# Residual rows of the last twelve chunks fetched by three large transfers, and the second sequence's statistics split over two steps

## Chip, cores and metric

One core of one Trainium2 chip runs the whole program. The metric is the device time of one execution in microseconds, and the median of several runs is given. Beside it stands one execution taken by the hardware profiler, whose span runs from its first to its last instruction.

## What is computed

Two sequences of 2048 tokens with 256 features pass through a recurrent layer and then through an attention layer with mixtures of experts for values and outputs. Both are added to their inputs. Cut to what matters here:

```python
x = x + rnn(layernorm(x), Wi, bi, Wh, bh)            # x: (2, 2048, 256)
y = layernorm(x)
q, k = heads(y @ Wq), heads(y @ Wk)                  # 8 heads of 64
wv = topk_mask(y @ Ws, 2) * sigmoid(y @ Ws)          # 5 experts, 2 taken
v = einsum('bthe,btek->bhtk', wv, einsum('btd,edk->btek', y, Wv))
attn = softmax(q * scale @ k.T) @ v
out = x + einsum('bthe,bthk,ekd->btd', topk_mask(y @ Wd, 2), attn, Wo)
```

The `x` of the last line, the output of the recurrent layer, is what this text calls the residual. The change concerns how its rows come back from memory for that last addition, and where the mean and variance for `layernorm(x)` of the second sequence are taken.

## The kernel before

The first 130 us hold the recurrent layer. Its result goes to a scratch tensor in memory, `x1d`, as 16 chunks of 128 rows for each of the two sequences (`b` is the sequence, `c` the chunk).

Attention follows, from about 130 us to the end. A *unit* is one head and one block of 512 queries: 8 heads by 4 blocks by 2 sequences make 64 units. A unit has eight tiles of scores (256 keys by 512 queries, held as 128 x 1024), which are treated in four *steps* `T` of two tiles, so there are 256 steps. In a step PE makes two tiles of scores `s` (L636); ACT copies them to a ring of tiles `p0` (even tiles) and `p1` (odd tiles, nine buffers; L648); DVE keeps the running maximum `m` (L658 to L664). When a unit's scores are complete, PE turns the maximum (`pm`, L677), DVE reduces it (`mq`, L682, `reduce_max`), and PE spreads it again (`pt`, L691, `spread_max`). Six steps behind (`LAG`), the maximum is subtracted by POOL or DVE (L704), ACT takes exponentials in place (L707), PE multiplies by the values (`o`, L717, `products`), POOL issues a DMA that adds the odd tile of a pair onto the even one (L729, `fold`; after it the `p1` tile is not needed any more), and PE sums the folded tiles over the keys (`d`, L738, `sums`). `take` and `take_sums` bring `o` and `d` to SBUF (`os`), and `close` divides and applies the output gates (`po` L770, `den` L772, `pro` L783); `gather` adds a head's share to what the other heads gave, for the last head on POOL (L840) into a tile `y` that `fetch_y` has loaded from memory (L804).

All instructions are in an order that is written by hand: the loop over `T` at the end of the kernel calls the pieces of a step in fixed order, and three tables of closures (`before`, `first_behind`, `behind`) say what else is called in a step and in which of its places. The engines run beside each other, each in its own order, with semaphores between them. SP issues nearly all other DMAs, also in program order, so an issue that must wait holds up those after it.

Two things lie beside that stream:

- Statistics of the second sequence. In the steps T = 15, 19, ..., 43, `stats_late` takes mean and variance of two chunks (L179 and L180 on DVE, four instructions in all), both at the end of the step, in `behind`. The rows are loaded by `load_late` (L886) one or two steps before. Step T = 19 and its like is the last of a unit (T % 4 == 3); the next step begins with that unit's `turn_max` and `reduce_max`.
- The output. When the last head of a query block is complete, `turn_out` transposes a chunk of `y` (`py`, L853), ACT copies it (`yT`, L857 and L860), a tile `z` of 128 x 256 (three buffers) is taken, and SP issues the load of the residual rows into it (L862, 128 KB). `project_out` multiplies by the output weights (`pz`, L870), DVE adds `z` (L878), and SP stores the result (L879). `pz` lies in one of two PSUM buffers that it shares with `po` and other small tiles.

The last three units end in `drain()`, a fixed list of calls after the loop. It holds the tail of the exponentials and products (`tv` and `tu` are the first tiles of the last two units), and the output of chunks 2 to 15 of the second sequence, in which a load of `z` stands in SP's order among the stores of earlier chunks.

Of the kernel before, what the change touches and what calls it, by code (L numbers as in the profile page):

```python
# [8 lines left out]
F32 = mybir.dt.float32  # L9
# [11 lines left out]
def rnn_then_switchhead_kernel(  # L21
# [658 lines left out]
    def reduce_max(u):  # L680
        pm, mq = mx_of[u]
        nc.vector.tensor_reduce(mq, pm, AX.X, ALU.max)  # L682

    def spread_max(u):
        _, mq = mx_of[u]
        if spare:
            pt = other(f"pt{u}_").rearrange("p (s q) -> p s q", q=P)
        else:
            pt = misc([P, QS, P], f"pt{u}")
        for s in range(QS):  # L690
            nc.tensor.transpose(pt[:, s, :], mq[:, s : s + 1].to_broadcast([P, P]), ident)  # L691
        pt = pt.rearrange("p s q -> p (s q)")
        if u in top_of:
            top_of[u] = (pt, top_of[u][1])
            return
        top_of[u] = (pt, ap.tile([P, QB], F32, tag="top", name=f"top{u}"))
        nc.scalar.copy(top_of[u][1], pt)  # L697
# [150 lines left out]
    def turn_out(b, c):  # L848
        yf = y_of[b, c // QS][:, c % QS].rearrange("p e k -> p (e k)")
        py = other(f"py{b}_{c}")[:, : len(o_chunks) * P] if spare else misc([P, len(o_chunks) * P], f"py{b}_{c}")  # L850
        py = py.rearrange("p (k n) -> p k n", n=P)
        for k, (r0, m) in enumerate(o_chunks):
            nc.tensor.transpose(py[0:m, k, :], yf[:, r0 : r0 + m], ident)  # L853
        yT = yT_all[yT_of["n"] % 2]
        yT_of["n"] += 1
        full = sum(m == P for _, m in o_chunks)
        nc.scalar.copy(yT[:, 0:full, :], py[:, 0:full, :])  # L857
        for k, (r0, m) in enumerate(o_chunks):
            if m < P:
                nc.scalar.copy(yT[0:m, k, :], py[0:m, k, :])  # L860
        z = ap.tile([P, D], F32, tag="z", bufs=3, name=f"z{b}_{c}")
        nc.sync.dma_start(out=z, in_=x1d[c, :, b, :])  # L862
        yT_of[b, c] = (yT, z)

    def project_out(b, c, at_end=False):
        yT, z = yT_of.pop((b, c))
# [69 lines left out]
        late["c"].pop(0)()  # L936


    before, first_behind, behind = {}, {}, {}

    def at(table, T, f, *a):
        table.setdefault(T, []).append(lambda: f(*a))
# [34 lines left out]
    for b in range(1, B):  # L977

        T0 = (b - 1) * H * H_T + 2 * LAG + 3
        for c in range(NCH):  # L980
            T = T0 + c // 2 * U_T
            at(behind, T - 2 + c % 2, load_late, b, c)
            at(behind, T, stats_late, b, c)
        T0 += NCH // 2 * U_T
        for part in range(2):
            at(behind, T0 + 3, scales_late, b, part)
            T0 += U_T
        for c in range(NCH):
            T = T0 + c // 2 * U_T + c % 2
            at(behind, T - 2, load_late, b, c)  # L990
            at(behind, T, normalize_late, b, c)
            at(behind, T + 2, turn_late, b, c)
            at(behind if c % 2 else before, T + 3, logits_late, b, c)
        T0 += 2 * NCH + U_T
        for part in range(2):
            for half in range(2):
                at(behind, T0, gates, b, part, half, False)
                for k in range(E):
                    at(behind, T0 + 1 + k, gates_go_on)
                T0 += 2 * U_T  # L1000
        assert T0 <= b * H * H_T
# [25 lines left out]
    def drain():  # L1027


        w, v, u = len(units) - 3, len(units) - 2, len(units) - 1  # L1030
        tv, tu = HC * v, HC * u
        outs = [(B - 1, c) for c in range(NCH)]
        turned, projected = 2, 1

        def turn(n=1):
            nonlocal turned
            for _ in range(n):
                turn_out(*outs[turned])
                turned += 1

        def project(n=1):
            nonlocal projected
            for _ in range(n):
                project_out(*outs[projected])
                projected += 1

        spread_max(v)
        turn_max(u)
        subtract(tv + 6, True)
        subtract(tv + 7)  # L1050
        reduce_max(u)
        take_sums(w)
        exponential(tv + 5)
        project()
        spread_max(u)
        products(tv + 4)
        products(tv + 5)
        fold(tv + 2)
        fold(tv + 4)
        exponential(tv + 6)  # L1060
        exponential(tv + 7)
        subtract(tu, True)
        close(w)
        gather(w)
        turn()
        exponential(tu)
        subtract(tu + 1, True)
        exponential(tu + 1)
        subtract(tu + 7)
        subtract(tu + 2, True)  # L1070
        products(tv + 6)
        products(tv + 7)
        fold(tv + 6)
        turn()
        project()
        take(v)
        sums(tv, tv + 2, True, False)
        exponential(tu + 2)
        subtract(tu + 3, True)
        exponential(tu + 3)  # L1080
        subtract(tu + 4, True)
        project()
        products(tu)
        products(tu + 1)
        turn()
        fetch_y(v)
        fold(tu)
        subtract(tu + 5, True)
        exponential(tu + 4)
        turn()  # L1090
        project()
        products(tu + 2)
        products(tu + 3)
        fold(tu + 2)
        sums(tv + 4, tv + 6, False, True)
        take_sums(v)
        exponential(tu + 5)
        subtract(tu + 6, True)
        turn()
        project()  # L1100
        exponential(tu + 6)
        products(tu + 4)
        products(tu + 5)
        exponential(tu + 7)
        turn()
        fetch_y(u)
        project()
        close(v)
        gather(v)
        products(tu + 6)  # L1110
        products(tu + 7)
        take(u)
        project()
        sums(tu, tu + 2, True, False)
        sums(tu + 4, tu + 5, False, False)
        sums(tu + 6, tu + 7, False, True)
        take_sums(u)
        turn()
        turn()
        project()  # L1120
        turn()
        project()
        turn()
        close_last(u, outs[-QS - 2 :])

    with tc.manual_schedule():
        for T in range(NT):
            new = (2 * T, 2 * T + 1)
            sub = [t for t in (2 * (T - LAG + 1), 2 * (T - LAG + 1) + 1) if 0 <= t < 2 * NT]
            old = [t for t in (2 * (T - LAG), 2 * (T - LAG) + 1) if 0 <= t < 2 * NT]  # L1130
            u_old = (T - LAG) // U_T - 1
            done = (T - LAG) % U_T == 0 and 0 <= u_old < len(units)
            fresh = sub and sub[0] % HC == 0
            if done:
                take(u_old)
            if old:
                exponential(old[1])

            ss = [scores(t) for t in new]
            stage(new[0], ss[0])  # L1140
            if T % U_T == 0:
                stage(new[1], ss[1])
                if T > 0:
                    turn_max(T // U_T - 1)
                    reduce_max(T // U_T - 1)
                largest(new[1], ss[1])
            else:
                largest(new[1], ss[1])
                stage(new[1], ss[1])
            if fresh:  # L1150
                subtract(sub[0])
            if T % U_T:
                largest(new[0], ss[0])
            if fresh:
                subtract(sub[1])
            k = T - LAG
            first = T % U_T == 0
            if first and k > 0:
                fold(2 * (k - 1))
            if sub and not fresh:  # L1160
                subtract(sub[0])
            if not first and k > 0:
                fold(2 * (k - 1))
            if sub and not fresh:
                subtract(sub[1])
            for f in before.pop(T, []):
                f()
            for t in old:
                products(t)
            if 3 <= k and k % 2:  # L1170
                t = 2 * (k - 3)
                sums(t, t + 2, t % HC == 0, t % HC != 0)
            if sub:
                exponential(sub[0])
            for f in first_behind.pop(T, []) + behind.pop(T, []):
                f()
        assert not before and not behind and not first_behind
        scores_only.close()
        spare["pool"] = ctx.enter_context(tc.tile_pool(name="ps_z", bufs=4, space=PSUM))
        drain()  # L1180


# [44 lines left out]
```

## Time and profile before

| quantity | us |
|---|---|
| median of 3 runs (1567.87 to 1571.04) | 1567.89 |
| the profiled execution's own time | 1569.4 |
| its span, first to last instruction | 1567.6 |
| PE busy | 1512.6 (96%) |
| DVE busy | 1299.1 (83%) |
| POOL busy | 1287.7 (82%) |
| ACT busy | 1247.8 (80%) |
| statistics of the second sequence on DVE | between 232.4 and 378.6 |
| start of the first projection inside `drain()` | 1513.0 |
| last residual addition | 1564.32 to 1564.74 |

PE is the matrix engine, DVE the vector engine, ACT the scalar engine, POOL GpSimd, and SP the queue that issues DMAs. An engine's busy time is an average over stages. What a piece of work costs is read from the stage that it stands in: from the idle time that the profile puts just before an instruction, in brackets, with the engine that ended it.

### The profile page before, as it was taken

To read this page: it belongs to the slowest core of one execution; us is meant where nothing else is said; L and a number is where in the kernel's file an instruction comes from. 1 tells how busy PE (TensorE), PEld (TensorE's weight loads), DVE (VectorE), ACT (ScalarE), POOL (GpSimd) and SP (SyncE) were. 2 spreads that over 40 slices of the span, in tenths; PEclk is the share of its full clock that TensorE was granted. 3 is DMA by queue.
4 is the path that set the end of the run, shared out by engine and by line. 5 is a ranking of instruction groups with operands and counts; after the bars stand their busy time and mean duration, and the time that the engine had idled before them with its cause. 6 is when DMAs were issued, how large, how long until landed. Compare 5 with 4: busy or idle time off the path is not lost. (4 is left out here: it accounts for less than half of the span.)

```text
span 1567.6 us, 41503 instructions
## 1 busy us (share of the span) xinstructions
PE 1512.6 (96%) x17582; PEld 533.7 (34%) x17582; DVE 1299.1 (83%) x1811; ACT 1247.8 (80%) x1617; POOL 1287.7 (82%) x855
## 2 busy tenths in 40 slices
PE   6988899999999999999999999999999999999997
PEld 5984222222233333333223332222222222222233
DVE  7473799999988888888987779999999999999873
ACT  4674688888888888888887778888888888888882
POOL 3053699898999988999998778899999999999980
PEclk9999999999999999999999999999999999999999
DMA  5021377888889987888897767788888888888955
GB/s 167 1 109 32 102 153 189 186 187 176 181 174 188 177 180 161 173 171 175 171 202 155 163 159 181 170 178 179 176 179 178 176 176 170 176 174 176 197 117 149
DMA packets 86959, 254.09 MB, mean 162 GB/s; under 512 B 11952, under 2 KB 31216, under 8 KB 86768
## 3 DMA queue, kind: packets, MB, share of 16 engines
q0 software_dynamic: 43488, 164.65, 57.5%
q1 hardware_dynamic: 41648, 86.13, 16.5%
q8 instruction: 139, 2.28, 0.6%
q10 hardware_dynamic: 1632, 0.61, 0.1%
q14 instruction: 52, 0.43, 0.1%
HBM read 59.46 MB, written 50.33 MB: 70 GB/s over the span
## 5 line engine op out<-in xcount | busy, mean ns | idle before, releaser
L704 POOL TENSOR_TENSOR p<-p,top 128x1024 f32<-128x1024 f32 x378 | 1006.3, 2768 | 27.9 <-ACT top L697 27.4
L648 ACT COPY p<-s 128x1024 f32<-128x1024 f32 x512 | 511.7, 1013 | 139.8 <-issue 49.5
L707 ACT ACTIVATE p<-p 128x1024 f32<-128x1024 f32 x512 | 538.8, 1063 | 50.7 <-DVE p L704 41.9
L636 PE MATMUL s<-q,k 64*32 64x512 f32 x4096 | 501.6, 596 | 3.6 <-ACT p L648 2.4
L636 PE MATMUL s<-qs,k 64*32 64x512 f32 x4096 | 501.4, 596 | 3.3 <-ACT p L648 1.8
L717 PE MATMUL o<-p,v 128*32 128x512 f32 x4096 | 491.0, 597 | 3.2 <-DVE os L754 2.3
L658 DVE TENSOR_TENSOR m<-s,m 128x1024 f32<-128x1024 f32 x320 | 390.9, 1222 | 89.4 <-PE s L636 80.8
L729 POOL DMA_DIRECT2D p<-p x254 | 263.0, 1036 | 97.6 <-issue 42.4
L717 PEld LDWEIGHTS o<-p,v 128*32 128x32 f32 x4096 | 113.5, 109 | 299.4 <-issue 158.0
L636 PEld LDWEIGHTS s<-qs,k 64*32 64x32 f32 x4096 | 100.3, 105 | 154.6 <-ACT p L648 58.2
L636 PEld LDWEIGHTS s<-q,k 64*32 64x32 f32 x4096 | 100.2, 105 | 153.9 <-ACT p L648 59.9
L704 DVE TENSOR_TENSOR p<-p,pt 128x1024 f32<-128x1024 f32 x126 | 152.5, 1210 | 0.0
L738 PE MATMUL d<-p,ones 128*32 128x512 f32 x1032 | 135.0, 592 | 0.9 <-DMA p<-p 0.9
L658 DVE TENSOR_TENSOR m<-s,p 128x1024 f32<-128x1024 f32 x64 | 78.4, 1225 | 57.5 <-ACT p L648 57.0
L783 DVE TENSOR_TENSOR pro<-po,mr 128x1280 f32<-128x1280 f32 (+1 forms) x67 | 95.9, 1431 | 2.7
L620 DVE TENSOR_TENSOR xq<-xq,wp 128x1280 f32<-128x1280 f32 x60 | 89.2, 1487 | 2.3 <-DVE wp L618 0.2
L626 DVE TENSOR_REDUCE v<-xq 128x256 f32<-128x1280 f32 x60 | 88.5, 1476 | 0.0
L159 PE MATMUL pq<-xn2T,wq 128*32 128x512 f32 x512 | 63.2, 612 | 6.4 <-DVE rtd L427 6.4
L140 PE MATMUL pk<-xn2T,wk 128*32 128x512 f32 x512 | 61.5, 597 | 0.0
L837 POOL DMA_DIRECT2D yd<-pro x48 | 61.0, 1270 | 0.0
L738 PEld LDWEIGHTS d<-p,ones 128*32 128x32 f32 x1032 | 33.9, 110 | 77.8 <-issue 75.8
L396 POOL TENSOR_TENSOR x<-x,hvb 128x512 f32<-128x512 f32 x14 | 17.9, 1276 | 45.8 <-ACT hs L369 34.2
(179 smaller groups left out, 1493.5 us busy)
## 6 DMA issues: line engine op xcount, KB each, us to landing
p<-p POOLq DMA_DIRECT2D x254, 512.0 KB, 5.4
xq<-xvd SPq DMA_DIRECT2D x60, 640.0 KB, 4.6
yd<-pro POOLq DMA_DIRECT2D x48, 640.0 KB, 6.5
qs<-q SPq DMA_DIRECT2D x64, 128.0 KB, 4.5
yd<-pro SPq DMA_DIRECT2D x8, 640.0 KB, 5.9
y<-yd SPq DMA_DIRECT2D x8, 640.0 KB, 7.3
x<-in_x SPq DMA_DIRECT2D x16, 256.0 KB, 5.5
x1d<-x SPq DMA_DIRECT2D x16, 256.0 KB, 2.0
```

The lines of the kernel that those rows point to most:

```text
L159: nc.tensor.matmul(pq[at_col : at_col + 32, :], lhsT=wq[:, kc, h * DH + g : h * DH + g + 32], rhs=xn2T[:, kc, b, n * QB : (n + 1) * QB], s ...
L620: nc.vector.tensor_tensor(xq, xq, wp.unsqueeze(2).to_broadcast([P, 4, DH, E]), ALU.mult)
L626: nc.vector.tensor_reduce(v_of[i][:, 4 * part : 4 * part + 4, :], xq, AX.X, ALU.add)
L636: nc.tensor.matmul(ss[g : g + 32, o, :], lhsT=k_of[i][half, c, g : g + 32], rhs=q_of[i, n][o][half, :], start=True, stop=True, tile_positi ...
L648: nc.scalar.copy(p, ss)
L658: nc.vector.tensor_tensor(m, ss, ring[t - 1] if c == 1 else m, ALU.max)
L704: eng.tensor_tensor(p, p, top.unsqueeze(1).to_broadcast([P, 2, QB]), ALU.subtract)
L707: nc.scalar.activation(ring[t], ring[t], AF.Exp)
L717: nc.tensor.matmul(o_of[u][at_col : at_col + 32, :], lhsT=v_of[i][:, 2 * c + o, g : g + 32], rhs=ring[t][:, o, :], start=c == 0, stop=c == ...
L729: nc.gpsimd.dma_start(out=ring[t], in_=ring.pop(t + 1), accum_op=ALU.add)
L738: nc.tensor.matmul(den_of[u][32 * g : 32 * (g + 1), :], lhsT=ones32, rhs=ring[(t, t1)[g // 2]][:, g % 2, :], start=first, stop=last, tile_ ...
L783: nc.vector.tensor_tensor(dst, po[:, s : s + n, 0:DH].unsqueeze(2).to_broadcast([P, n, E, DH]), mr[:, s : s + n].unsqueeze(3).to_broadcast ...
```

## The change

Residuals: a new function `load_z` takes one buffer of the ring `p1` and loads four chunks of residual rows (512 KB) into it with one DMA. It is called three times in `drain()`: twice at its start, for chunks 4 to 7 and 8 to 11, and once after the second projection in the list, for chunks 12 to 15. `turn_out` uses a slice of such a tile where there is one, and takes a `z` tile and loads it as before otherwise (chunks 0 to 3 of this sequence and everything earlier). The buffers are those whose tiles are folded last: the three calls take the ones of the tiles folded in step 254, in step 255, and by the first `fold` in `drain()`. In the same list `fetch_y(v)`, the load of `y` for chunks 8 to 11, stands one turn and two projections earlier.

Statistics: a new table `between` has a place just before `largest(new[1], ...)`, and in the first step of a unit this is behind `reduce_max`. The even chunk of a pair is measured there in the step T of before (the last of a unit), the odd one there in the next step, behind the maximum of the finished unit.

The instructions of PE, ACT and POOL and their order are the same in both kernels. On DVE the statistics move; on SP twelve loads go, three come, and one moves.

```diff
@@ turn_out
-        z = ap.tile([P, D], F32, tag="z", bufs=3, name=f"z{b}_{c}")
-        nc.sync.dma_start(out=z, in_=x1d[c, :, b, :])
+        z = yT_of.pop(("z", b, c), None)
+        if z is None:
+            z = ap.tile([P, D], F32, tag="z", bufs=3, name=f"z{b}_{c}")
+            nc.sync.dma_start(out=z, in_=x1d[c, :, b, :])
         yT_of[b, c] = (yT, z)
+
+    def load_z(b, n):
+
+        z = ap.tile([P, QS, D], F32, tag="p1", bufs=RING[1], name=f"zz{b}_{n}")
+        nc.sync.dma_start(out=z, in_=x1d[n * QS : (n + 1) * QS, :, b, :].rearrange("c p d -> p c d"))
+        for s in range(QS):
+            yT_of["z", b, n * QS + s] = z[:, s, :]
@@ the table of the second sequence
             at(behind, T - 2 + c % 2, load_late, b, c)
-            at(behind, T, stats_late, b, c)
+            at(between, T + c % 2, stats_late, b, c)
@@ drain
+        load_z(B - 1, NQ - 3)
+        load_z(B - 1, NQ - 2)
         spread_max(v)
         turn_max(u)
         subtract(tv + 6, True)
...
         fold(tv + 6)
         turn()
+        fetch_y(v)
         project()
+        load_z(B - 1, NQ - 1)
         take(v)
         sums(tv, tv + 2, True, False)
...
         products(tu + 1)
         turn()
-        fetch_y(v)
         fold(tu)
@@ the loop over T
                 if T > 0:
                     turn_max(T // U_T - 1)
                     reduce_max(T // U_T - 1)
+                for f in between.pop(T, []):
+                    f()
                 largest(new[1], ss[1])
             else:
+                for f in between.pop(T, []):
+                    f()
                 largest(new[1], ss[1])
                 stage(new[1], ss[1])
```

More of the change, by code (lines that the diff above doesn't have):

```diff
@@ L936, in gates_go_on @@
         late["c"].pop(0)()
-    before, first_behind, behind = {}, {}, {}
+    before, between, first_behind, behind = {}, {}, {}, {}
     def at(table, T, f, *a):
@@ L1176, in rnn_then_switchhead_kernel @@
                 f()
-        assert not before and not behind and not first_behind
+        assert not before and not between and not behind and not first_behind
         scores_only.close()
```

## The prediction, on record before the changed kernel ran

> **What bounds the kernel now.** I read the page first, then the waits of each engine in the last 57 us, the timelines of DVE and SP there, the end of the chain, and then the groups and timelines of the steps with statistics beside units without them.
>
> ```profile
> PE 1512.6 (96%) x17582; PEld 533.7 (34%) x17582; DVE 1299.1 (83%) x1811; ACT 1247.8 (80%) x1617; POOL 1287.7 (82%) x855
> ```
>
> PE is the bound: in the middle a PE gap is time, and an idle DVE is not. So I look for PE's gaps in the two stages that the change touches, and for what stands between PE's last matmul and the end. The waits of PE from 1511 us on:
>
> ```profile
> PE po L770 <- DVE z L878: 2.5, 1, 2.5
> PE py L853 <- POOL y L840: 0.9, 1, 0.9
> PE pz L870 <- DVE den L772: 0.5, 1, 0.5
> PE pz L870 <- ACT yT L857: 0.4, 2, 0.2
> ```
>
> The first is at 1539.12: `po` needs the PSUM buffer of the projection of chunk 5, and DVE has not added the residual to it. DVE's timeline and SP's say why:
>
> ```profile
> 1526.41 1.21 DVE L704 TENSOR_TENSOR p<-p,pt__17190 128x1024 f32<-128x1024 f32 x1
> 1534.50 0.42 DVE L878 TENSOR_TENSOR z<-pz,z 128x256 f32<-128x256 f32 x1 [6.88 <-issue]
> 1538.63 0.42 DVE L878 TENSOR_TENSOR z<-pz,z 128x256 f32<-128x256 f32 x1 [1.76 <-DMA z<-x1d]
> ...
> 1522.55 4.30 SPq L879 DMA_DIRECT2D out<-z  x2
> 1526.95 1.15 SPq L862 DMA_DIRECT2D z<-x1d  x1
> 1528.20 0.98 SPq L804 DMA_DIRECT2D y<-yd  x1
> ```
>
> The projection of chunk 4 is done at 1528.3, but its residual, behind a store on SP, is only asked for at 1526.95 and takes 7.5 us: 1534.45. Everything behind it on DVE is late: the sums of L761, a subtraction (1535.65), two exponentials, `po`, the gated `pro`, and with it POOL's addition (1544.19 to 1547.10) that `py` waits for. The end of the chain is the same:
>
> ```profile
> 1561.80 2.33 DMA z<-x1d
> ...
> 1564.32 0.42 DVE z L878
> ```
>
> PE's last projection ends at 1562.90, yet the addition starts at 1564.32, on a residual asked for at 1561.80.
>
> In the steps with statistics, PE waits once a unit before it spreads the maximum:
>
> ```profile
> 255.75 0.65 PE L691 MATMUL pt<-ident,mq 128*128 128x128 f32 x4 [0.39 <-DVE mq L682]
> 253.09 0.42 DVE L179 BATCH_NORM_STATS2 stl<-xl 128x6 f32<-128x256 f32 x1
> 269.17 1.23 DVE L658 TENSOR_TENSOR m<-s,m 128x1024 f32<-128x1024 f32 x1 [0.66 <-PE s L636]
> 1407.50 1.23 DVE L658 TENSOR_TENSOR m<-s,m 128x1024 f32<-128x1024 f32 x1 [0.66 <-PE s L636]
> 1414.44 1.22 DVE L658 TENSOR_TENSOR m<-s,p 128x1024 f32<-128x1024 f32 x1 [0.77 <-ACT p L648]
> ```
>
> The four statistics instructions (from 253.09 to 254.25) stand ahead of `mq`, and `pt` waits 0.39 for it. The last two lines are a unit without statistics: no wait at `pt`, and DVE has two idle places, 0.66 before the maximum of the last step and 0.77 before the first maximum of the next unit. The windows between turned maxima:
>
> ```profile
> 252.85:273.58 20.73, 20.27 (x244) 5.82 (x236) 19.40 (x26) 17.84 (x21) 18.44 (x11) 1.00 0.88 210
> 1391.60:1411.91 20.31, 20.23 (x244) 5.81 (x237) 18.37 (x22) 17.65 (x21) 18.51 (x12) 1.00 0.87 176
> ```
>
> First length, then PE, PEld, DVE, ACT and POOL busy. PE's work is equal, the length differs by 0.42.
>
> [...] for 6.88 us DVE leaves L761 and L704 undone that need no residual. [...] The trace has 2.1 to 2.6 for a quiet residual and 4.1 for a quiet `y`, but up to 9.2 and 9.8 beside other traffic. [...] the trace has 424 for L878 and 406 for L179.
>
> **The change part by part.**
>
> *Residuals.* Out: twelve loads of 128 KB; in: three of 512 KB, the same bytes, into buffers that are free. SP gets 9 issues fewer (0.32 to 1.18 us each), which is off the path.
> When do they land? The first waits for the fold of step 254, issued at 1503.49 and landed 4.6 later, so for nothing; it goes behind the load of chunk 1, at 1512.6. The second waits for the fold of step 255 (1508.80 + 4.8 = 1513.6; I take 1514.5, as the first transfer runs beside it). Duration: a quiet 128 KB takes 2.3, a quiet 640 KB 4.1, so 512 KB about 3.7 (an estimate between these rows); beside traffic up to 9.8. I take 4 to 6: chunks 4 to 7 are there by 1518, chunks 8 to 11 by 1521, both before the first need at 1528.3. The third goes out behind a store at about 1522.9 and is needed after 1556.
> Then the 6.88, 1.76, 2.52 and later residual waits of DVE go. What is late next? PE up to 1536.57 has no gap above 0.2 and stays. After that:
> - `po` follows the projection of chunk 6 at once: -2.54. Its `os` is ready, since L761 moves to about 1531.6. The subtraction and two exponentials behind it end by about 1536, before the products that need them (1537.1; before, 1539.70).
> - The projection of chunk 7 waits 0.53 for the residual addition of chunk 6; gone.
> - `py` waits 0.93 for POOL. Now `pro` runs 1537.9 to 1539.4, POOL 1539.4 to 1542.3, and PE gets there at 1542.9: gone, with 0.6 to spare. POOL needs `y` of chunks 8 to 11, now asked for at about 1520.4 behind the transpose of chunk 3; with 9.8 us it lands at 1530.
> - The sums before that need the fold issued at 1529.77, which took 11.2 beside `y` and two residuals, to 1541.0. PE now wants it at about 1540.1. `y` and the residuals are no longer beside it, so 5 to 7 us, 1536; had it stayed at 11.2, it would take back 0.9.
> - From `py` on PE runs without gaps to its end, 4.0 earlier (1558.9), and the last addition follows 0.07 behind it, as at 1549.79, instead of 1.42: -1.35. `y` of the last unit is asked for behind the transpose of chunk 7 (1535.1) and needed at 1549.8.
> Sum: 2.54 + 0.53 + 0.93 + 1.35 = 5.35.
> What the new traffic costs: 1 MB between 1512.6 and 1520, with the folds issued at 1514.07 and 1516.83 and the residuals of chunks 2 and 3 (4.0 and 7.4 us), which are behind the large transfers on SP. Chunk 2 landed at 1520.1 and is added at 1522.11; chunk 3 at 1524.6, added at 1526.07; the first fold at 1519.4, summed at 1521.61. All have 1.5 to 2.2 us to spare, and the DMA is idle from 1514 to 1516. The extra is 1 MB at about 290 GB/s (108 GB/s at a DMA share of 0.37 after 1550), 3.6 us, of which 2 lie in that idle stretch. So the loss is between 0 and 1.6 past these margins for PE; below nothing is excluded, since nothing that PE waits for in that stretch comes earlier. I take 0.4.
>
> *Statistics.* The same 32 instructions. The even pair (0.42 and 0.18, and 0.65 to the next start as at 253.64 to 254.29) goes into the idle 0.66 before L658 in the last step. If it is over by some tenths, the maximum, ACT's copy and PE's next scores follow: at 414.75 a row of small instructions made that maximum late by about 0.97, and PE lost 0.73, so 0.24 is free. The odd pair goes into the 0.77 behind `mq`: 0.65 fits, and if not, DVE comes to the next idle place (0.66) a little later. Nothing of ACT or POOL waits for statistics; of SP only the load that reuses the tile, a step ahead of its need. So the waits at `pt` of eight units go: 0.38, six of 0.39, 0.73, sum 3.45. In the first of these the idle place is only 0.26 (227.78): 0.65 - 0.26 - 0.24 = 0.15 comes back; I take 0.2 for the other margins, 0.02 and 0.12 wide. Gain 3.1, between 1.5 (the even pair disturbs half as much) and 3.4.
>
> *Together:* 5.35 - 0.4 + 3.1 = 8.1 (rounded up from 8.05). Against the profiled span 1567.6 this is 1559.5, and for its own time 1569.4 it is 1561.3; the median of the runs shown, 1567.89, is 0.3 above the span, so 1567.9 - 8.1 = 1559.8.
>
> **The rivals.**
> 1. *The traffic takes the place of the late residual.* A fold or the residual of chunk 2 lands 2 to 4 us late, and PE stalls in 1521 to 1530. For it: a DMA share of about 1.0 from 1516 to 1522, one landing of 11.2. Against: the idle stretch. 1567.9 - 3.1 - (5.35 - 3) = 1562.4.
> 2. *The statistics only change place.* The margin of 0.01 before L658 does not hold, and PE waits at its scores instead of `pt`. For it: the row at 414.75. Against: there it was 1.72 us of instructions, not 0.65. 1567.9 - 4.95 = 1562.9.
> 3. *Slower.* SP stands at the second large transfer. Its issue waits for the fold of step 255 and for other completions of POOL's DMAs; if one of these is the fold issued at 1516.83 (landed at 1524.4), or the transfers crawl, the residual of chunk 2 goes out behind it. Each us that it lands after 1522.4 stops DVE, with the subtractions, exponentials and products behind it, by one us. It must land at 1530.5 to eat up the 8.1: 1524.4 plus 6. With 9.2 us it lands at 1533.6, cost 11.2: 1571.0. Against: only earlier folds can have had that buffer.
> 4. *The residuals still come late*, since the large transfers are held up but chunk 2 is not: the statistics alone, and a rest, 1565.
>
> **How the numbers follow.** Forecast 0.66; rival 1 0.15; rival 2 0.10; rival 3 0.04; rival 4 0.05. The range goes from both gains whole and half a us more (1567.9 - 8.8 - 0.5 = 1558.6, and below it to 1558.0 for waits that I have not summed) to the upper end of rivals 1 and 2, 1563.5. This kernel's measurement can tell about 0.2%, 3.1 us, from no change: faster means below 1564.8. That is the forecast and rivals 1 and 2 (0.91), less a little for stalls that add up: faster 0.90, same 0.06, slower 0.04.
>
> **What would show it.** Right: no residual wait above 0.5 on DVE after 1515; `po` directly behind `pz`; last addition within 0.1 of PE's end; units of about 20.3 from 232 to 398; no PE wait at `pt` there. Wrong: PE waits before `d` or `o` around 1520 to 1530, PE waits at L636 in those units, or an SP wait above 5 us at the second large load.

## The result, and the profile after

| | before | after |
|---|---|---|
| median of six runs on one chip, us | 1569.11 (1567.87 to 1571.04) | 1563.84 (1560.75 to 1564.61) |
| profiled execution's own time, us | 1569.4 | 1563.39 |
| its span, us | 1567.6 | 1561.6 |
| its mean granted clock | 0.997 | 0.995 |

The ratio is 0.9962 with an interval of 0.9949 to 0.9975: 6.0 us faster, 3.9 to 8.0 (the two medians differ by 5.3). The forecast was 8.1 faster, a little outside that interval, and its time of 1559.8 is 4.0 below the median measured. Of these 4.0, 1.2 is the kernel before itself, whose median was 1567.89 in the three runs shown ahead of the prediction and 1569.11 in six. The stated range ended at 1563.5, and the median of 1563.84 lies 0.3 above it; 0.9962 of the 1567.89 that it was reckoned from is 1561.9, inside the range. In what follows the differences count.

First PE's share of the span on the page of the changed kernel, then the list of all waits of PE in its end stage, from 1503 us on (engine, line, what it waited for: us in total, times, longest):

```profile
PE 1514.2 (97%) x17582; PEld 535.3 (34%) x17582; DVE 1299.9 (83%) x1811; ACT 1245.5 (80%) x1617; POOL 1287.0 (82%) x855
```
```profile
PE d L738 <- DMA p<-p: 0.7, 1, 0.7
PE pz L879 <- ACT yT L857: 0.5, 2, 0.3
```

The waits of 2.5 at `po`, 0.9 at `py` and 0.5 at `pz` that were listed before are gone. One is new: `d`, the sums over the keys, waits 0.7 for a fold. The timelines of DVE, PE and SP in that stage (start, duration, instruction, and in brackets the idle time before it):

```profile
1526.30 0.42 DVE L887 TENSOR_TENSOR zz<-pz,zz 128x256 f32<-128x256 f32 x1 [0.79 <-PE pz L879]
...
1558.24 0.42 DVE L887 TENSOR_TENSOR zz<-pz,zz 128x256 f32<-128x256 f32 x1 [0.87 <-PE pz L879]
```
```profile
1527.76 1.03 PE L738 MATMUL d<-p,ones 128*32 128x512 f32 x4
1529.50 1.05 PE L738 MATMUL d<-p,ones 128*32 128x512 f32 x4 [0.71 <-DMA p<-p]
...
1534.59 1.50 PE L879 MATMUL pz<-wo,yT 128*32 128x256 f32 x24
1536.02 0.66 PE L770 MATMUL po<-ident,os 128*128 128x128 f32 x4
...
1555.37 2.80 PE L879 MATMUL pz<-wo,yT 128*32 128x256 f32 x48
```
```profile
1510.87 1.16 SPq L870 DMA_DIRECT2D zz<-x1d  x2
...
1520.95 1.32 SPq L870 DMA_DIRECT2D zz<-x1d  x1
```

The 6.88, 1.76 and later waits of DVE for residual rows are gone: chunk 4's addition, which came at 1534.50, is at 1526.30 and waits for PE alone. `po` follows its `pz` at once. The last addition starts at 1558.24, 0.07 behind PE's last matmul (1555.37 + 2.80). SP issued both large loads in 1.16, so it did not stand at the second. But where the kernel before had one group of eight `d` matmuls, there are two groups of four with a gap: the fold of the second half had not landed. The group of before, and POOL's issue of the same fold there (the first of the two):

```profile
1529.87 1.07 PE L738 MATMUL d<-p,ones 128*32 128x512 f32 x8
```
```profile
1525.27 1.76 POOL L729 DMA_DIRECT2D p<-p  x2
```

The chain of work that ended last in the changed kernel passes through the fold:

```profile
1523.16 6.29 DMA p<-p
...
1555.44 2.77 PE pz L879 x48
...
1558.24 0.42 DVE zz L887
```

It took 6.3. The fold of the same tile took 4.6 before and landed at 1529.87, just when PE began these sums: it had no time to spare. And it costs more than the wait of 0.71 that the list shows: all eight matmuls took 1.07 together, and now each four take as long by themselves, so the sums are done 2.79 after their start (1527.76 to 1530.55), 1.72 later than before.

The statistics, on DVE in two steps of one unit, and the windows between turned maxima, the same two units as in the prediction (length, then busy PE, PEld, DVE, ACT, POOL, clock, DMA share, GB/s):

```profile
249.18 0.42 DVE L179 BATCH_NORM_STATS2 stl<-xl 128x6 f32<-128x256 f32 x1
249.92 1.23 DVE L658 TENSOR_TENSOR m<-s,m 128x1024 f32<-128x1024 f32 x1
...
256.12 0.43 DVE L179 BATCH_NORM_STATS2 stl<-xl 128x6 f32<-128x256 f32 x1
256.87 1.23 DVE L658 TENSOR_TENSOR m<-s,p 128x1024 f32<-128x1024 f32 x1
```
```profile
254.33:274.71 20.38, 20.28 (x245) 5.83 (x237) 19.50 (x26) 17.64 (x21) 18.52 (x11) 1.00 0.88 211
1391.60:1411.91 20.31, 20.23 (x242) 5.83 (x236) 18.37 (x21) 17.64 (x21) 18.53 (x12) 1.00 0.88 176
```

The maximum follows each pair without a gap, `pt` (at 256.77) has no wait, and the unit is 20.38 long where it was 20.73. From the turned maximum at 211.06 to the one at 397.89, the kernel before took 186.83; after, 212.68 to 396.64 is 183.96: 2.87 gained.

I measure the end stage from the start of `o` in step 254 to the start of the last residual addition. Before: 1503.42 to 1564.32, 60.90. After: 1501.30 to 1558.24, 56.94. Gain 3.96. These two gains make 6.8; the rest of the span brings the balance to 6.0, since the first 212 us, in which both kernels have the same instructions, took 1.6 longer in the profiled execution of after (its granted clock is 0.69 from 24 to 26 us and 0.50 from 26 to 28, where before has 1.00), and the stretch between the two stages 0.9 less.

### The profile page after: what moved, and what is told of

The parts are those of the page before. It is cut to its first block, busy times and chain, and to the rows that moved or that the text cites. A ratio compares the mean times of both kernels' runs of the same rounds, so it can differ in the third digit from the quotient of the medians.

```text
span 1561.6 us, 41489 instructions
## 1 busy us (share of the span) xinstructions
PE 1514.2 (97%) x17582; PEld 535.3 (34%) x17582; DVE 1299.9 (83%) x1811; ACT 1245.5 (80%) x1617; POOL 1287.0 (82%) x855
## 4 chain that ended last, share of the span: by engine, by line
PE 59%; DVE 19%; ACT 7%; issue 5%; DMA 2%; POOL 1%; ACTq 0%; DVEq 0%; POOLq 0%
PE s L636 22%; PE o L717 17%; DVE m L658 10%; ACT p L648 5%; PE d L738 4%; PE pq L159 4%; DVE pro L783 4%; PE pk L140 3%; PE pz L879 3%; DMA p<-p 2%; ACT p L707 1%; PE pv L575 1%; PE py L853 1%; PE pt L691 1%; PE pvf L575 1%
```

## The experiments

The theory after the result: the statistics gain about what was forecast; the residual waits are gone as forecast (5.35); and the new traffic, put at 0.4, costs some 2 us because it makes folds and residuals land late. The rivals: statistics that merely change place; one transfer alone (the third large load, or `y`) that is to blame; a fold that is issued too late. Every edit below is made to the changed kernel. With all waits taken out that the prediction named, the end stage is 60.90 - 5.35 = 55.55; what a stage is longer than that is the cost of traffic.

**Statistics alone.** The drain of before.

```diff
-        load_z(B - 1, NQ - 3)
-        load_z(B - 1, NQ - 2)
...
-        fetch_y(v)
         project()
-        load_z(B - 1, NQ - 1)
...
         turn()
+        fetch_y(v)
```

> The statistics moved as in the changed kernel, the residuals loaded as before. Theory (the two parts add up, each in its own stage): no wait of PE at pt between 232 and 398 us, units there of 20.3 us, and the time falls by 2.9 us (the stretch from the turned maximum at 211 to the one at 398 got 2.87 shorter in the changed kernel); the end stage after the last scores is that of before, with its waits of 2.5, 0.9 and 0.5. Rival (the statistics only change place, and the whole gain is in the end stage): within 0.5 us of before.

1567.69 against 1570.15: 0.9985 (0.9976 to 0.9993), a gain of 2.4 us (1.1 to 3.8). Units from 211.04 to 395.03, 183.99, without a wait at `pt`; end stage 60.58 with its old waits (2.80 at `po` for a residual addition, 2.54 before; behind it the clock is 0.50 from 1538 to 1540).

The statistics do not merely change place: their trace gain of 2.84 is there without the residuals' change.

**Residuals alone.** The statistics where they were before.

```diff
-            at(between, T + c % 2, stats_late, b, c)
+            at(behind, T, stats_late, b, c)
```

> The residuals loaded as in the changed kernel, the statistics where they were. Theory: the waits of 0.38 to 0.73 at pt in eight units stay, and the stretch from the first projection inside the end stage to the last residual addition is about 4 us shorter than before, with one wait of PE at d for a fold; the time falls by 4.0 us, and this and the statistics alone add up to the changed kernel's gain within 1 us. Rival (the parts are worth something only together): the sum misses it by more than 2 us.

1568.16 against 1570.15: 0.9986 (0.9979 to 0.9993), a gain of 2.2 us (1.1 to 3.3). The waits at `pt` are back, the units take 186.84, the end stage 56.67. The two halves together make 4.6 in the timed runs, and the whole 6.0: equal within what the intervals tell. The half that falls short is this one: the forecast gave it 4.95, the expectation 4.0, and 3.3 is the most that its interval allows. The profiled execution shows 4.2 in the stage (60.90 - 56.67), but its whole span is only 2.3 shorter. The other 1.9 went ahead of the stage, where the instructions are those of before: 0.6 in the first 212 us, and 1.3 between 398 and the stage, where PE waits 2.0 for a fold at one place (0.9 before). So executions differ there too, and one profile of each kernel does not tell the gain.

**The third large load later**, behind the sums instead of ahead of them.

```diff
-        load_z(B - 1, NQ - 1)
         take(v)
...
         take_sums(v)
+        load_z(B - 1, NQ - 1)
```

> The changed kernel with the third large load (chunks 12 to 15) called only behind take_sums of the last unit but one. In the changed kernel PE waits before the second half of d for the fold of tv + 6, which took 6.3 us instead of 4.6, and the work behind it is 1.7 us later. Theory 1 (the third large transfer, on its way from 1521 to 1527, crowds that fold): the fold lands within 5 us, PE's wait goes, and the time is 1.5 us below the changed kernel. Theory 2 (the earlier y, on its way from 1518 to 1525, does): no change, the wait of 0.7 stays.

0.9963 (0.9948 to 0.9977), median 1563.40. In the trace the fold that was late lands after 5.1 instead of 6.3, `d` is one group (1.62), and the stage is 55.77, 1.17 shorter than after. The time cannot tell this from the changed kernel (0.9962), though 1.5 less had been expected.

**`y` at its old place.**

```diff
-        fetch_y(v)
         project()
...
         turn()
+        fetch_y(v)
```

> The changed kernel with the load of y for chunks 8 to 11 back at its old place, behind the transpose of chunk 4. Theory 1 (the third large transfer crowds the fold of tv + 6): the wait of PE at d stays, no gain, since y, now asked for at about 1525, is beside the fold too. Theory 2 (the earlier y does): the fold lands within 5 us and the time is 1.5 us below the changed kernel. In both y lands before POOL needs it at 1539.

0.9959 (0.9944 to 0.9973), median 1564.28. The fold takes 5.7, `d` is one stretched group of 2.15, the stage 56.30. So each of the two transfers may have a part in the late fold, and neither alone is shown to be it: the same code as the changed kernel's gave 6.0 to 6.3 in the three executions that had no stop ahead of this fold, and 5.7 is not far from that.

**The fold earlier.** POOL's subtraction that stood ahead of the fold goes behind it.

```diff
-        subtract(tu + 7)
         subtract(tu + 2, True)
...
         fold(tv + 6)
+        subtract(tu + 7)
```

> The changed kernel with POOL's subtraction of tile tu + 7 called behind the fold of tv + 6 instead of ahead of it, so that this fold is issued about 2.4 us earlier, at 1520.8 on the time axis of the changed kernel. Theory (what is lost in the end stage is that fold's landing, whatever crowds it): it lands before 1528 even if it takes 7 us, PE does not wait at d, and the stage from the products of step 254 to the last residual addition, 60.9 before and 56.9 in the changed kernel, falls to 55.2. Rival (another wait stands right behind it): stays above 56.3.

1566.79 against 1571.08: 0.9972 (0.9963 to 0.9981). PE's timeline:

```profile
1532.72 1.05 PE L738 MATMUL d<-p,ones 128*32 128x512 f32 x4 [1.33 <-DMA p<-p]
```

The fold was issued 19.5 after the stage's start instead of 21.9, and took 9.3 instead of 6.3. The wait grew from 0.71 to 1.33 and the stage is 57.56. The theory that the fold is issued too late fell: the DMA engines were full (shares of 1.02, 0.95 and 1.07 from 1515 to 1525, on to 1530 and on to 1535), and here the earlier issue was not an earlier landing.

**Twelve small loads** in the place and buffers of the large ones, four of 128 KB for each.

```diff
-        nc.sync.dma_start(out=z, in_=x1d[n * QS : (n + 1) * QS, :, b, :].rearrange("c p d -> p c d"))
         for s in range(QS):
+            nc.sync.dma_start(out=z[:, s, :], in_=x1d[n * QS + s, :, b, :])
             yT_of["z", b, n * QS + s] = z[:, s, :]
```

> The changed kernel with each large load split into four loads of 128 KB into the same tiles, at the same places. Theory 1 (early request into free buffers is what counts, not the size): no residual wait for chunks 4 to 15, the stage is between 56.5 and 58; what remains is SP's time, 5 more issues by 0.4 to 0.7 us before the loads of chunks 2 and 3, which may make the addition of chunk 2 up to 2 us late. Theory 2 (one large transfer is what counts): residual waits of over 1 us on DVE come back for chunks 4 to 7, and the stage is above 59.

1565.58 against 1571.08: 0.9971 (0.9960 to 0.9982). SP and DVE:

```profile
1509.84 4.73 SPq L871 DMA_DIRECT2D zz<-x1d  x8
```
```profile
1522.38 0.42 DVE L887 TENSOR_TENSOR z<-pz,z 128x256 f32<-128x256 f32 x1 [3.30 <-DMA z<-x1d]
```

Chunks 4 to 15 have no wait here either, so it is the early buffers and not the size of a transfer that removed the waits. But eight issues hold SP for 4.73 instead of 1.16, chunk 2's own load goes out behind them, and the stage is 59.58 (as long as the other theory had it, for another reason): PE's `o` waits 2.81 and then takes 3.10 at a clock of 0.82 to 0.50. Fewer issues do count when a needed load stands behind them.

**Even chunks alone at the new place.**

```diff
-            at(between, T + c % 2, stats_late, b, c)
+            at(behind if c % 2 else between, T, stats_late, b, c)
```

> The changed kernel with only the even chunk's statistics at the new place, the odd one's at the end of the step as before, ahead of the reduction of the maximum. Theory (PE waits at pt only for the part of 1.2 us that goes beyond DVE's slack there, 1.20 - 0.39 = 0.81): one pair takes 0.60, no wait at pt, and the stretch between the turned maxima at 211 and 398, 186.8 before and 184.0 in the changed kernel, is again 184.0. Rival (each pair costs PE its share): 185.4.

0.9957 (0.9942 to 0.9971), median 1565.03. The units take 184.09: moving one of two chunks brings 2.74 of the 2.87. The wait at `pt` was only 0.38 or 0.39 in seven of the eight units, and one chunk (0.65) is more than that (of the 0.73 in the eighth, 0.2 is left); what counts is that the rest fits, not how much is moved. The drain is that of after, yet its stage is 59.37. DVE's timeline:

```profile
1525.65 0.42 DVE L887 TENSOR_TENSOR z<-pz,z 128x256 f32<-128x256 f32 x1 [4.62 <-DMA z<-x1d]
```

Here chunk 2's residual, which stands behind the large loads, took 10.6 (5.9 after), and DVE with all that stands behind it waited 4.62; PE's `o` then waits 1.86. The profiled run, 1566.77, was the slowest of the kernel's four; the others were 1562.32 to 1565.76. One code has several outcomes.

**Both chunks at the even place**, ahead of the last step's maximum.

```diff
-            at(between, T + c % 2, stats_late, b, c)
+            at(between, T, stats_late, b, c)
```

> The changed kernel with both chunks' statistics at the even one's place, before the maximum in the last step of a unit. Theory (the cover there is DVE's idle 0.66 and 0.24 behind it): two pairs take 1.20, so PE loses about 0.3 at its scores in each of eight units and some more in the first, and the stretch is 186.3 to 186.9, nearly all of the gain of the statistics gone. Rival (the place has more cover than that): 184.0.

1593.61 against 1571.08: 1.0140 (1.0125 to 1.0155), slower by 22 us, which neither theory expected. DVE, PE and SP:

```profile
255.02 0.43 DVE L179 BATCH_NORM_STATS2 stl<-xl 128x6 f32<-128x256 f32 x1 [4.71 <-DMA xl<-x1d]
```
```profile
257.91 1.08 PE L636 MATMUL s<-qs,k 64*32 64x512 f32 x4 [4.89 <-ACT p L648]
```
```profile
248.43 0.47 SPq L170 DMA_DIRECT2D qs<-q  x1
...
249.63 0.55 SPq L895 DMA_DIRECT2D xl<-x1d  x1
```

The odd chunk's rows are asked for only at 249.63, behind copies of queries in SP's order, and land about when DVE takes them at 255.02; DVE stands there ahead of the maximum, and PE's scores wait 4.89. So this run priced a load and not the operations. It also shows what the split by `T + c % 2` rests on, which the prediction left out when it named only the load that reuses the tile: the odd chunk cannot be measured one step earlier unless its load moves.

**The same with both loads one step earlier**, three steps ahead of the unit's last.

```diff
-            at(behind, T - 2 + c % 2, load_late, b, c)
-            at(between, T + c % 2, stats_late, b, c)
+            at(behind, T - 3, load_late, b, c)
+            at(between, T, stats_late, b, c)
```

> Both chunks' statistics at the even one's place once more, but both loads called three steps ahead, so that they go out on SP before the copies of the next queries and not behind them. With the odd load one step ahead DVE waited 4.7 for it in every second unit. Theory 1 (that load was the whole loss but for what the place cannot cover): no wait for a load, and what is left is the 1.20 of DVE work against a cover of 0.66 and 0.24, 0.3 in each of eight units and some more in the first: the stretch between the turned maxima is 186.3 to 186.9 (184.0 in the changed kernel, 186.8 before). Theory 2 (the place has more cover): 184.0 to 185.

1567.29 against 1569.88: 0.9981 (0.9973 to 0.9990). No wait for a load; the units take 186.51, so that only 0.3 of the gain of 2.87 is left. On DVE both pairs now stand ahead of the maximum:

```profile
247.90 0.42 DVE L179 BATCH_NORM_STATS2 stl<-xl 128x6 f32<-128x256 f32 x1
...
248.98 1.19 DVE L658 TENSOR_TENSOR m<-s,m 128x1024 f32<-128x1024 f32 x1
```

One pair fits into the idle 0.66 there, two (1.08, from 247.90 to 248.98) do not. That is the cover that the prediction named, measured from its other side. The end stage of this execution, again with the drain of after, was 59.91. DVE waited 3.52 in it for chunk 2's residual. PE's timeline, and the windows with the granted clock (third number from the end):

```profile
1527.42 3.37 PE L717 MATMUL o<-p,v 128*32 128x512 f32 x16 [2.39 <-DVE os L754]
```
```profile
1527.00:1529.00 2.00, 1.58 (x12) 0.69 (x16) 1.97 (x3) 0.44 (x1) 0.00 (x0) 0.69 1.08 204
1529.00:1531.00 2.00, 2.00 (x13) 0.34 (x6) 2.00 (x3) 0.62 (x1) 0.86 (x1) 0.50 0.93 159
```

The sixteen matmuls behind the stop take 3.37, where they take 1.92 after. The granted clock fell to 0.50 behind the stop: the shares 0.69, 0.50 and, from 1531 to 1533, 0.96 are 1.7 us of lost PE work. Here the late landing cost its wait and then this.

**The two first large loads behind chunk 3's turn**, so that chunks 2 and 3 are asked for first.

```diff
-        load_z(B - 1, NQ - 3)
-        load_z(B - 1, NQ - 2)
...
         turn()
+        load_z(B - 1, NQ - 3)
+        load_z(B - 1, NQ - 2)
         fetch_y(v)
```

> The changed kernel with the first two large loads called behind the transpose of chunk 3 instead of at the start of the end stage, so that the small residual loads of chunks 2 and 3 go out ahead of them. With the same end stage, four profiled executions so far gave 56.7, 56.9, 58.0 and 59.4 us from the products of step 254 to the last addition, with the addition of chunk 2 waiting up to 4.6 for its residual. Theory (the two large transfers at the start are what makes chunk 2's residual and the next fold late): no residual wait for chunk 2 and no wait of PE at the first d; the stage is 55.5 to 57.2, the later fold of tv + 6 may still cost up to 1.8. Rival (those waits come from the folds themselves, as the two transfers have landed by then): chunk 2 waits again in some execution, and the stage stays between 56.7 and 59.4.

1567.52 against 1570.73: 0.9978 (0.9969 to 0.9987), less gain than the changed kernel in the same session (0.9963). Chunk 2 is on time and the first fold takes 5.4. But the large loads take 8.0 and the third 15.5, the fold that was 6.3 takes 7.9, and the stage is 60.17:

```profile
1532.40 1.05 PE L738 MATMUL d<-p,ones 128*32 128x512 f32 x4 [2.31 <-DMA p<-p]
```

The crowd has only moved to where `d` is, and the stage is longer than either theory had it. From 1533 to 1538 the granted clock is 0.68 and 0.65, another 1.7 of PE's work lost behind this stop.

**Spread.** Each large load goes out near its need: the first behind chunk 3's turn, the second behind the sums, the third behind `gather(v)`; `y` at its old place.

```diff
-        load_z(B - 1, NQ - 3)
-        load_z(B - 1, NQ - 2)
...
-        fetch_y(v)
+        load_z(B - 1, NQ - 3)
         project()
-        load_z(B - 1, NQ - 1)
...
         turn()
+        fetch_y(v)
...
         take_sums(v)
+        load_z(B - 1, NQ - 2)
...
         gather(v)
+        load_z(B - 1, NQ - 1)
```

> The changed kernel with its large loads spread: the first behind the transpose of chunk 3, the second behind take_sums of the last unit but one, the third behind that unit's gather, and the load of y at its old place. Theory (1.6 MB asked for between 1510 and 1527 is what fills the DMA engines, and each of these transfers is needed much later): no wait of PE for a fold, no residual wait above 0.5, stage 55.2 to 55.9, and the time is 1 to 3 us below the changed kernel's on the same chip. Rival (the folds crowd each other): stage above 56.7.

1562.56 against 1570.73: 0.9950 (0.9938 to 0.9962), a gain of 7.8 us (6.0 to 9.7). `d` has no wait, and the stage is 55.72. The windows from 1510 to 1530 of before, after and this kernel (columns as above; DMA share and GB/s are the last two):

```profile
1510.00:1530.00 20.00, 19.71 (x220) 8.52 (x215) 14.73 (x20) 13.11 (x23) 13.63 (x9) 1.00 0.73 155
```
```profile
1510.00:1530.00 20.00, 19.00 (x205) 8.02 (x203) 13.71 (x18) 12.00 (x21) 12.17 (x9) 1.00 1.03 267
```
```profile
1510.00:1530.00 20.00, 19.71 (x229) 8.31 (x231) 14.82 (x20) 13.25 (x22) 11.36 (x8) 1.00 0.86 180
```

In the changed kernel the DMA engines are busy from one end of these 20 us to the other; with the loads spread they are not, and PE's busy time is back at 19.71. Only the later sums are stretched, 3.31 instead of 2.76, since a fold took 10.7 beside the second load.

**The changed kernel once more**, in the same session as the last two.

> The changed kernel itself once more, beside the two others on the same chip. It gives a further sample of the end stage: theory (its length depends on how the transfers happen to meet in an execution), between 56.7 and 59.4; the time 0.9962 of before, within the interval of the first measurement.

1564.36 against 1570.73: 0.9963 (0.9950 to 0.9976); stage 56.68. The result repeats. The spread kernel's median is 1.8 below it, but the intervals overlap: that it beats the changed kernel is likely and not shown, that it beats the kernel before is.

## Why the prediction was right in its mechanism and off in one term

*Residual waits, 5.35: right.* The 2.54, 0.53, 0.93 and 1.35 are gone from the lists of waits after. A stage of 55.72 with the loads spread is within 0.2 of the 55.55 that the sum asks for. The estimate of 4 to 6 us for a large load held in the changed kernel: 4.2 to 5.0 for the first two, 5.9 for the third.

*Statistics, 3.1: right.* 2.87 in the trace of after, 2.84 with the statistics alone; 2.4 (1.1 to 3.8) timed. Of the waits of 3.45, some 0.6 came back where the prediction allowed 0.35; no single wait of PE shows it. The cover was priced rightly on both sides: one pair in the idle 0.66 costs PE nothing visible, two pairs take back 2.6 of the gain. (The margin given as 0.02 is 0.66 - 0.65 = 0.01; nothing hangs on it.)

*"What the new traffic costs … I take 0.4": the step that failed.* The margins of 1.5 to 2.2 us for chunk 2, chunk 3 and the first fold were differences of times from a single execution, with the landing times of a quieter DMA (chunk 2 took 4.0 there, and 5.6 to 10.6 in the six executions below). And the list of transfers in danger ended with the first fold, while in the profiled execution it was a later one, issued at 1523.16, that landed late; in the kernel before it had landed with no margin. So one of the prediction's own signs of being wrong came, PE's wait before `d`, beside all its signs of being right. Six profiled executions ran the drain of after:

| kernel | stage, us | above 55.55 | largest waits of PE in it (all at a clock of 1.00 but the last) |
|---|---|---|---|
| changed | 56.94 | 1.4 | 0.71, `d` for a fold |
| residuals alone | 56.67 | 1.1 | 0.45, `d` for a fold |
| changed, repeated | 56.68 | 1.1 | 0.34, `d` for a fold |
| both at the even place | 58.03 | 2.5 | 2.07, `o` behind chunk 2 |
| even chunks alone | 59.37 | 3.8 | 1.86, `o` behind chunk 2; 1.26, `d` |
| both, loaded early | 59.91 | 4.4 | 2.39, `o` behind chunk 2 |

Their mean is 2.4 above 55.55. The timed runs agree in size: 5.35 + 3.1 - 6.0 is 2.4 for the whole change, and 5.35 - 2.2 is 3.2 (2.1 to 4.3) for the residuals alone, where 0.4 had been put. But they do not say where it was lost, and part of it need not be in this stage, since stretches with the same instructions differ as well. The turned maximum near 212 us comes at 210.8 to 211.6 in seven of the fourteen profiled executions and at 212.5 to 213.2 in the other seven; both of the changed kernel are among the late ones, the one of before is not. In the late one of after the granted clock is 0.50 from 26 to 28 us, and the eight matmuls of `px` from 24 us on take 2.97; in two more late ones (third large load later, `y` at its old place) they take 3.50 and 3.15, and in before and in each half alone 1.89. And between 800 and 1000 us PE waits 0.9 for a fold in before, 0.6 in after and 2.0 with the residuals alone.

What was lost in the stage is rival 1's mechanism (forecast 5.5 for the whole gain; measured 6.0), and in the executions with chunk 2 late also rival 3's place, but with SP never standing at the second load (1.16 for the two issues of after; that the second waits for further completions of POOL's DMAs was an assumption of that rival and is not shown): chunk 2's rows were not asked for late, they landed after 9.2 to 10.6 instead of 5.9. The rivals "only change place" and "still late" are refuted by the waits and the units' lengths.

What made the estimate small: it counted the extra megabyte against an idle stretch of 2 us and subtracted. The windows show what that leaves out. At 155 and 267 GB/s the 20 us moved some 3.1 MB before and 5.3 after, so 2.2 MB were added, with `y` and the third load brought forward, and not 1. They fill both idle stretches of before (1514 to 1516, and 1524 to 1526), the DMA share is 1.03, and transfers that are needed first land later too.

Rival 3 priced a late microsecond at one microsecond. That term, too, could be small: in the last row of the table the wait of 2.39 is followed by 1.7 of lost PE work.

*Open.* Why the transfers of the same code crowd more in one execution (59.91) than in another (56.67) is not settled. They are asked for at the same times: in all six executions SP issues the large loads 9.5 to 9.6 us after the stage's start and chunk 2's load 12.7 after it, and yet chunk 2 lands after 5.6 to 6.1 in three of them and after 9.2 to 10.6 in the other three. What decides it these traces do not show. The kernels differ ahead of the drain only in where the statistics and their loads stand, a thousand us earlier. How often an execution loses clock in this stage is not known either, since only profiled executions show the stage. That a later third load or an older place for `y` is faster by itself was not told apart by the times.

## What to carry to other kernels

A load that is asked for early is not free: it takes its place among transfers that somebody needs sooner (behind the two large loads chunk 2 landed after 5.6 to 10.6 us here, and after 4.0 without them). Ask for each piece near its need and not for all in one crowd (the right order alone, in one crowd, gave less here: 0.9978 against 0.9963; spread it was 0.9950), and look at the DMA share of the stretch into which a load is moved; where that comes to 1.0 (1.03 here), margins read off a quiet execution are worth little, and the range should take in a few executions. Where PE stops for as long as in these end stages, look at the granted clock behind the stop as well as at the stop: of the six stops of 2.07 to 2.81 us four (2.31, 2.39, 2.80 and 2.81) were followed by about 1.7 us of lost work. A small operation belongs into an idle place of its engine that is longer than it is (0.66 for 0.65 here), ahead of which its own data has landed: the load's place in its queue has to move with it (DVE stood 4.71 for rows whose load had not moved).

## What the runs showed of the hardware that was not expected

- A 512 KB load took 3.9 us (even chunks alone) to 5.3 (changed, repeated) at the head of the stretch, and beside other traffic 11.5 (spread, the second) and 15.5 (behind chunk 3, the third). A fold of 512 KB took 4.5 to 11.9 in the execution of before, 5.4 in the median of its 254.
- A fold issued 2.4 us earlier, into DMA engines that were full (1.02 from 1515 to 1525), landed about 0.6 later against the stage's start in the one execution seen (19.5 + 9.3 against 21.9 + 6.3).
- The granted clock fell behind stops of PE of 2.31, 2.39, 2.80 and 2.81 us, and stayed at 1.00 behind those of 1.86 and 2.07 and behind the 2.54 of before. The lowest windows show 0.65 behind the stop of 2.31 and 0.50 behind the three longer ones, and each of the four cost about 1.7 us of PE's work (two windows of 2 us at 0.69 and 0.50 and one at 0.96, for the 2.39). As 2.31 was followed by it and 2.54 was not, the length of the stop alone does not tell when it comes; what does, these traces do not show.
- In the run with both chunks at the even place, the score groups behind each of PE's four stops of 4.88 to 5.27 took 1.08 instead of 0.63 (the granted clock is 0.50 from 258 to 263, behind the first of these stops), and the mean granted clock was 0.988; the other profiles had 0.995 to 0.998.
- Executions of one kernel scatter: 43 of the kernel before, taken beside the statistics alone, lie between 1567.84 and 1574.44. In the runs of the statistics alone, a mean granted clock of 0.992 went with 1573.06, and 0.997 with 1566.3 in the mean of ten.
